# Layer 1's values two key blocks at a time beside layer 2, in a four-layer attention kernel

## The chip, the cores and the metric

The kernel runs on one core of a Trainium2 chip. Such a core has a matrix engine (TensorE, PE in the profile, with PEld for its loads of weights), a vector engine (VectorE, DVE), an engine for functions such as the exponential (ScalarE, ACT), a general one (GpSimd, POOL), and queues for transfers (SP issues nearly all of them here). Matrix products are written to a small memory of their own, PSUM; everything else is in SBUF. The metric is the time of one execution on the device in microseconds (us); the number given for a kernel is the median of several runs.

## The reference

The input x is four images of 64 x 64 pixels with 64 channels, all float32. Four layers follow one another, and each is an attention of every pixel over pixels of the same image, with a residual:

```python
# layer 0: q, k, v = x@Wq, x@Wk, x@Wv;  attn = softmax(q k^T, over keys)
out = einsum('bmn,bmc->bnc', attn, v);  x = gamma*out + x
# layer 1: theta = x@w_theta (8 columns); phi, g = maxpool2(x@w_phi), maxpool2(x@w_g)  (8 and 32 columns)
attn = softmax(einsum('bnd,bmd->bnm', theta, phi));  x = x + sigma*((attn g)@w_o + b_o)
# layer 2: group norm of 32 groups, q, k, v; softmax over keys; projection; + residual
# layer 3: group norm of 8 groups, q, k, v; softmax over keys; projection; + the normed input
```

Layers 0, 2 and 3 have 4096 queries and 4096 keys of 64 channels per image. Layer 1 pools its keys to 1024, and its queries and keys have only 8 channels, its values 32. Its four weights are first divided by an estimate of their largest singular value.

## The kernel before

All the work is written for one core, in an order fixed by hand (`tc.manual_schedule()`, L623): each engine carries out its instructions in the order in which the program issues them. The semaphores between engines follow from what reads and writes which tile.

Images lie channel by channel, two halves of 64 channels on the 128 partitions. Tiles come from pools (L625 to L627): `x` for what is as large as an image (8 KB a partition; the images themselves, q, k, v, layer 1's th, pg and its sums zacc1), `p` for exponentials (4 KB a partition), `ps_s` with two PSUM buffers of 128 x 1024 for scores and for everything else that is short-lived, and `ps_a` with four banks of 128 x 512 for accumulated outputs. A tile that is asked for when all buffers of its pool are taken waits for the last reader of one of them.

The large attentions (layers 0, 2 and 3) run one after another. Each is a loop of 64 steps, `step()` (L816). In layers 2 and 3 (`attention`, L1270) a step issues, in this order: two units of scores (`first`, matmuls at L1286 into both buffers of `ps_s`, each followed by an exponential on ACT, L1291, and a sum on DVE, L1297), and then the values' products of two units of an earlier step (`then`, L1321, into two `ps_a` banks).

The small work runs beside these loops as a generator that yields at named places (`background`, L782; `advance`, L806): MID lies between the two units of values, LATE in the middle of the second one, END after the step. At LATE the second unit of values is split by columns into two halves (`parts`, L846): the first half, then the background's piece, then the second half. When the second unit is a chunk's first or last key block, it isn't split, and the background's piece comes behind it.

Layer 1 is such a background. For images 1, 2 and 3 it runs beside layer 2 of the image before (L1777, L1783, L1789, with `bank=True`), and for image 0 beside layer 0 of image 1 (L1774, `bank=False`). Its loop (L1202 to L1217) goes over 16 units (two halves j of the queries, eight key blocks k each), in n = 0 to 16, one n at a LATE:

- `scores` (L1112) issues eight matmuls (L1120; the trace counts each float32 matmul twice, so 16) that fill both buffers of `ps_s`, and two exponentials on ACT (L1126) that empty them into two tiles of `p`. The array of TensorE is tiled 32 x 64 for them, as the keys have only 8 channels.
- `add` (L1139) multiplies the exponentials of one unit by its values, four matmuls (L1146, 8 in the trace) in a tiling of 128 x 32, into one `ps_a` bank that collects all eight key blocks of a half. After the eighth block ACT copies the bank.
- `accumulate` (L1133) sums the exponentials on DVE (L1135, x2 per unit); beside layer 2 it is put off to the end of the step (`later`).

In each n of 1 to 15, `scores` of unit n is followed by `add` of unit n - 1; n = 0 has only scores, and n = 16 only the last `add`. With `bank=False` the `add` comes at END instead, into a `ps_s` buffer.

Of the kernel before, what the change touches and what calls it, by code (L numbers as in the profile page):

```python
# [597 lines left out]
def fast_path(tc: tile.TileContext, a: dict, out: bass.AP, bad, read_flag):  # L598
# [10 lines left out]
    x = a["x"]  # L609
# [10 lines left out]
    MID, ALONE, LATE, END = range(4)  # L620
# [2 lines left out]
    ctx.enter_context(tc.manual_schedule())  # L623
    pool = lambda name, bufs, **kw: ctx.enter_context(tc.tile_pool(name=name, bufs=bufs, **kw))
    const, small = pool("const", 1), pool("small", 2)  # L625
    x_p, p_p, z_p, o_p = pool("x", 13), pool("p", 14), pool("z", 2), pool("o", 2)
    ps_s, ps_a = pool("ps_s", 2, space=PSUM), pool("ps_a", 4, space=PSUM)  # L627

    s_tile = lambda: ps_s.tile([P, 1024], FP, tag="s", name="s")
# [432 lines left out]
    def layer1(on, st, bank):  # L1062
# [49 lines left out]
        def scores(j, k):  # L1112

            ss = [s_tile() for e in range(2)]
            n, d = divmod(k, 2)
            for m in range(2):
                for e in range(2):
                    for i in range(2):
                        r = slice((2 * e + i) * 32, (2 * e + i) * 32 + D8)
                        nc.tensor.matmul(  # L1120
                            ss[e][half(m), chunk(i)], pgs[0 if e == d else 1][r, ds(n * P + m * C, C)],
                            th[r, chunk(i ^ j)], start=True, stop=True,
                        )
            ps[j, k] = pk = [p_tile() for e in range(2)]
            for e in range(2):
                nc.scalar.activation(pk[e], ss[e], AF.Exp)  # L1126
            if k == 0:
                return lambda: None
            if k == 1:
                zaccs[j] = x_tile("zacc1").rearrange("p (e f) -> p e f", e=2)  # L1130
            zs = [ps[j, 0][e] if k == 1 else zaccs[j][:, e, :] for e in range(2)]

            def accumulate():  # L1133
                for e in range(2):
                    nc.vector.tensor_tensor(zaccs[j][:, e, :], zs[e], pk[e], ALU.add)  # L1135

            return accumulate

        def add(j, k):  # L1139
            if k == (NK - 1 if bank else 0):  # L1140
                os[j] = o_tile("o1")
            if k == 0 and bank:
                accs[j] = acc_tile()
            acc = accs[j] if bank else s_tile()[:, 0:512]
            for q in range(4):
                nc.tensor.matmul(  # L1146
                    acc[quarter(q), :], g[:, k, :], ps[j, k][q // 2][:, chunk(q % 2)],
                    start=(k == 0 or not bank), stop=(k == NK - 1 or not bank),
                )
            if k > 0:  # L1150
                del ps[j, k]
            if k == 1:
                del ps[j, 0]
            if not bank and k > 0:
                nc.vector.tensor_tensor(os[j], os[j], acc, ALU.add)  # L1155
            elif not bank or k == NK - 1:
                nc.scalar.copy(os[j], acc)
# [44 lines left out]
        todo = [(j, k) for j in range(2) for k in range(NK)]  # L1202
        for n in range(len(todo) + 1):
            accumulate = None
            if n < len(todo):
                yield LATE
                accumulate = scores(*todo[n])
            if n:
                if not bank:
                    yield END  # L1210
                elif n == len(todo):
                    yield LATE
                add(*todo[n - 1])
            if accumulate and bank:
                later.append(accumulate)
            elif accumulate:
                accumulate()  # L1217
# [554 lines left out]
    layer0(s0)  # L1772
    drain()
    background(3.0, layer1("DVE", s0, False), before2("DVE", s0))  # L1774
    free = layer0(s1)
    drain()
    background(3.0, layer1("ACT", s1, True), before0("ACT", s2))  # L1777
    free = layer2(s0, free)
    drain()
    background(1.0, before2("DVE", s1), loads(s3))  # L1780
    free = layer0(s2)
    drain()
    background(3.0, layer1("ACT", s2, True), before0("ACT", s3))  # L1783
    free = layer2(s1, free)
    drain()
# [52 lines left out]
def conv_seq_kernel(tc: tile.TileContext, a: dict, out: bass.AP):  # L1838

    nc = tc.nc  # L1840
    with tc.tile_pool(name="flag", bufs=1) as flag:
        bad = flag.tile([1, 1], I32, name="bad")
        n_bad = fast_path(tc, a, out, bad, lambda: nc.values_load(
            bad[0:1, 0:1], min_val=0, max_val=128, skip_runtime_bounds_check_because="it is a count of 128 partitions"
        ))
        with tc.If(n_bad > 0):
            general_path(tc, a, out)
# [37 lines left out]
```

## Time and profile before

| | us |
|---|---|
| median of three runs (lowest, highest) | 2929.19 (2929.1, 2929.22) |
| the profiled execution, its own time | 2929.51 |
| its span, from the first to the last instruction | 2927.8 |
| PE busy | 2896.2 |
| DVE busy | 1869.1 |
| ACT busy | 1799.6 |
| stretches with layer 1 beside layer 2, near | 563 to 666, 1059 to 1161, 1555 to 1658 |
| PE, DVE, ACT busy in those three together (308 us) | 305.81, 253.09, 208.26 |
| a usual step there; a step of layer 2 without layer 1 | 5.64; 3.43 |

The profile is of one execution. Its page gives each engine's busy time, then the chain of waits that ended last (by engine and line), then groups of instructions. The timeline lists instructions in order of time, and those alike and overlapping are merged, with their number behind an x. In brackets stands how long an engine was idle before, and what ended that. PE's instructions overlap: the time that a group costs is read from its start to the start of the next group. The granted clock of TensorE is 0.999 throughout.

### The profile page before, as it was taken

The page shows a single profiled execution, that of the slowest core. Times are in us where ns is not written, and L with a number is a line of the kernel's source. Part 1 is how long each engine was busy: PE and PEld are TensorE (multiplying, and loading weights), DVE is VectorE, ACT ScalarE, POOL GpSimd, SP SyncE. Part 2 cuts the span into 40 slices and gives each one's busy share as a digit, 9 for nine tenths or more (in the row PEclk, how much of TensorE's full clock was granted, in tenths as well). Part 3 has the DMA queues.
Part 4 walks back from the last instruction along what each step waited for, and adds up shares of the span by engine and source line. Part 5 has one row for each costly group of instructions (what it writes and reads, how often), then busy time and mean ns, then how long its engine had stood idle before and what let it go on. Part 6 is the DMA issues. An engine that isn't in the chain of part 4 may idle for free.

```text
span 2927.8 us, 66456 instructions
## 1 busy us (share of the span) xinstructions
PE 2896.2 (99%) x29413; PEld 1135.3 (39%) x29413; DVE 1869.1 (64%) x2145; ACT 1799.6 (61%) x2481; POOL 33.7 (1%) x33
## 2 busy tenths in 40 slices
PE   9999999999999999999999999999999999999998
PEld 3333233333444433344443334444344444443333
DVE  2112752589831078973017998888888877878878
ACT  5666666665566766556766655555555655655554
POOL 0000000000000000000000000000000000000000
PEclk9999999999999999999999999999999999999999
DMA  2010000000002000000000000000000000000000
GB/s 38 1 30 5 1 1 16 5 5 5 19 5 30 1 5 5 11 17 16 1 1 5 5 9 20 19 5 9 5 19 7 21 5 7 6 20 5 8 5 9
DMA packets 76776, 30.11 MB, mean 10 GB/s; under 512 B 70464, under 2 KB 74560, under 8 KB 75072
## 3 DMA queue, kind: packets, MB, share of 16 engines
q1 hardware_dynamic: 74224, 25.37, 4.6%
q8 instruction: 232, 3.80, 0.5%
q10 hardware_dynamic: 2256, 0.41, 0.1%
q14 instruction: 64, 0.52, 0.1%
HBM read 4.79 MB, written 4.19 MB: 3 GB/s over the span
## 4 chain that ended last, share of the span: by engine, by line
PE 93%; DVE 4%; ACT 1%; issue 1%; DVEq 0%; ACTq 0%
PE acc L1321 28%; PE s L1286 28%; PE s L999 15%; PE acc L1028 15%; DVE zacc L1297 3%; PE s L1120 2%; PE acc L1146 2%; ACT p L1126 1%; PE s L1146 1%; PE s L912 0%; PE s L891 0%; PE s L1417 0%; PE s L1092 0%; PE s L1465 0%; PE s L1437 0%
## 5 line engine op out<-in xcount | busy, mean ns | idle before, releaser
L1291 ACT ACTIVATE p<-s 128x1024 f32<-128x1024 f32 x1024 | 994.4, 1022 | 693.6 <-PE s L1286 666.9
L1297 DVE TENSOR_TENSOR zacc<-zacc,p 128x1024 f32<-128x1024 f32 x960 | 1174.3, 1223 | 182.5 <-ACT p L1291 119.3
L1321 PE MATMUL acc<-p,v 64*64 64x512 f32 (+1 forms) x8576 | 1008.7, 572 | 0.0
L1009 ACT ACTIVATE p<-s 128x1024 f32<-128x1024 f32 x480 | 486.9, 1020 | 115.0 <-PE s L999 114.9
L1321 PEld LDWEIGHTS acc<-p,v 64*64 64x64 f32 x8576 | 349.2, 133 | 532.9 <-issue 532.9
L1028 PE MATMUL acc<-p,vs 64*64 64x512 f32 (+1 forms) x4224 | 502.0, 578 | 0.0
L1286 PE MATMUL s<-q,k 64*64 64x512 f32 x2048 | 492.1, 591 | 2.1 <-ACT p L1126 2.1
L1286 PE MATMUL s<-q,xT 64*64 64x512 f32 x2048 | 490.5, 590 | 0.0
L999 PE MATMUL s<-xT,q 64*64 64x512 f32 x2048 | 487.9, 592 | 2.5 <-DVE mean L1353 0.7
L999 PE MATMUL s<-xT,q_swapped 64*64 64x512 f32 x2048 | 488.1, 592 | 0.3 <-DVE o L1155 0.3
L1286 PE MATMUL s<-q,k_swapped 64*64 64x512 f32 x2048 | 481.2, 591 | 2.1 <-DVE xT L1471 2.1
L1286 PE MATMUL s<-q,h_swapped 64*64 64x512 f32 x2048 | 479.5, 590 | 0.5 <-DVE mean L1353 0.2
L1011 DVE TENSOR_REDUCE all_z<-z 128x1 f32<-128x4 f32 x128 | 20.1, 157 | 607.3 <-ACT p L1009 607.1
L1028 PEld LDWEIGHTS acc<-p,vs 64*64 64x64 f32 x4224 | 174.2, 133 | 264.7 <-issue 262.9
L1286 PEld LDWEIGHTS s<-q,h_swapped 64*64 64x64 f32 x2048 | 150.3, 133 | 135.6 <-issue 127.3
L1286 PEld LDWEIGHTS s<-q,k_swapped 64*64 64x64 f32 x2048 | 148.0, 133 | 140.7 <-issue 86.2
L1286 PEld LDWEIGHTS s<-q,xT 64*64 64x64 f32 x2048 | 150.7, 133 | 133.0 <-issue 127.1
L999 PEld LDWEIGHTS s<-xT,q_swapped 64*64 64x64 f32 x2048 | 146.9, 133 | 140.2 <-issue 111.2
L999 PEld LDWEIGHTS s<-xT,q 64*64 64x64 f32 x2048 | 144.7, 133 | 140.1 <-issue 108.9
L1286 PEld LDWEIGHTS s<-q,k 64*64 64x64 f32 x2048 | 148.6, 133 | 116.8 <-issue 98.2
L1017 ACT ACTIVATE vs<-v,all_r 128x64 f32<-128x64 f32 x256 | 89.0, 348 | 158.4 <-PE acc L1028 81.0
L1126 ACT ACTIVATE p<-s 128x1024 f32<-128x1024 f32 x128 | 124.1, 1021 | 82.8 <-PE s L1120 82.8
(215 smaller groups left out, 1322.7 us busy)
## 6 DMA issues: line engine op xcount, KB each, us to landing
k_swapped<-k SPq DMA_DIRECT2D x8, 512.0 KB, 6.3
residual<-turned SPq DMA_DIRECT2D x128, 32.0 KB, 1.8
h_swapped<-xT SPq DMA_DIRECT2D x8, 512.0 KB, 6.3
out_dram<-turned SPq DMA_DIRECT2D x60, 64.0 KB, 2.0
xin<-in_x_dram SPq DMA_DIRECT2D x12, 256.0 KB, 6.6
q_swapped<-q SPq DMA_DIRECT2D x6, 512.0 KB, 7.0
pg<-pg SPq DMA_DIRECT2D x8, 128.0 KB, 2.3
xin<-in_x_dram SPq DMA_DIRECT2D x12, 64.0 KB, 2.2
```

The costliest lines, as they stand in the source:

```text
L999: nc.tensor.matmul(s[half(e), chunk(i)], queries(m, i, e), k[half(i), chunk(c)], start=True, stop=True)
L1009: nc.scalar.activation(p, s, AF.Exp, accum_out=z)
L1011: nc.vector.tensor_reduce(zsum[:, m : m + 1], zs.pop(m), AX.X, ALU.add)
L1017: nc.scalar.activation(vs, v[:, m, :], AF.Copy, scale=rz[:, m : m + 1])
L1028: nc.tensor.matmul(acc[c][half(i), cols], scaled[t][half(e), :], ps[NC * m + c][half(e), chunk(i)][:, cols], start=(m == 0 and not second) ...
L1120: nc.tensor.matmul(ss[e][half(m), chunk(i)], pgs[0 if e == d else 1][r, ds(n * P + m * C, C)], th[r, chunk(i ^ j)], start=True, stop=True,)
L1126: nc.scalar.activation(pk[e], ss[e], AF.Exp)
L1146: nc.tensor.matmul(acc[quarter(q), :], g[:, k, :], ps[j, k][q // 2][:, chunk(q % 2)], start=(k == 0 or not bank), stop=(k == NK - 1 or not ...
L1286: nc.tensor.matmul(s[half(e), chunk(i)], k[(j + i) % 2][half(i), ds(j // 2 * P + e * C, C)], q[half(i), chunk(c)], start=True, stop=True,)
L1291: nc.scalar.activation(p, s, AF.Exp)
L1297: add = lambda: nc.vector.tensor_tensor(zaccs[c], p0, p, ALU.add)
L1321: nc.tensor.matmul(accs[c][e][half(i), cols], v[half(e), j, :], p[half(e), chunk(i)][:, cols], start=(j == 0), stop=(j == NB - 1),)
```

## The change

Where layer 1 runs beside layer 2, `add` is called for two units in succession at every even n (n = 2, 4, ..., 16, for units n - 2 and n - 1), behind the scores of that n, and not at all at odd n. The exponentials of an even unit are thus kept a step longer. The pool of exponentials has 16 buffers for 14, the pool of images 12 for 13 (the same space in all: 8 KB a partition less, 8 KB more). Layer 1 of image 0 (`bank=False`) is as before, except that the condition is written the other way round.

```diff
-    x_p, p_p, z_p, o_p = pool("x", 13), pool("p", 14), pool("z", 2), pool("o", 2)
+    x_p, p_p, z_p, o_p = pool("x", 12), pool("p", 16), pool("z", 2), pool("o", 2)
...
             if n < len(todo):
                 yield LATE
                 accumulate = scores(*todo[n])
-            if n:
-                if not bank:
-                    yield END
-                elif n == len(todo):
+            if n and not bank:
+                yield END
+                add(*todo[n - 1])
+            elif n and n % 2 == 0:
+
+                if n == len(todo):
                     yield LATE
-                add(*todo[n - 1])
+                for unit in todo[n - 2 : n]:
+                    add(*unit)
             if accumulate and bank:
                 later.append(accumulate)
             elif accumulate:
```

## Prediction

> **What bounds the kernel now.** I read the page first (busy shares, the chain of waits, the costliest groups), then the timeline of TensorE beside layer 2, then that of all engines there.
>
> ```profile
> span 2927.8 us, 66456 instructions
> PE 2896.2 (99%) x29413; PEld 1135.3 (39%) x29413; DVE 1869.1 (64%) x2145; ACT 1799.6 (61%) x2481; POOL 33.7 (1%) x33
> ...
> PE 93%; DVE 4%; ACT 1%; issue 1%; DVEq 0%; ACTq 0%
> ```
>
> The reader is to see that TensorE (PE) is busy for 99% and carries 93% of the chain: what an edit adds to PE, or leaves PE waiting for, is added to the time. So I ask of each step beside layer 2 how long it is on PE and why. The first timeline is PE alone, in the first two steps in which layer 1's loop runs beside layer 2 (columns: start, length, engine, line, operation; an entry's length includes the overlap with the next, so I go by differences of starts).
>
> ```profile
> 564.02 1.11 PE L1120 MATMUL s<-th,pg 8*64 8x512 f32 x16
> 565.07 0.66 PE L1321 MATMUL acc<-p,v 64*64 64x256 f32 x8
> 566.29 0.65 PE L1286 MATMUL s<-q,k 64*64 64x512 f32 x2 [0.56 <-ACT p L1126]
> ...
> 568.11 1.47 PE L1321 MATMUL acc<-p,v 64*64 64x512 f32 x16
> 569.51 1.11 PE L1120 MATMUL s<-th,pg 8*64 8x512 f32 x16
> 570.55 1.07 PE L1146 MATMUL acc<-p,pg 128*32 128x512 f32 x8
> 571.55 0.66 PE L1321 MATMUL acc<-p,v 64*64 64x256 f32 x8
> 572.03 0.60 PE L1286 MATMUL s<-q,k 64*64 64x512 f32 x2
> ...
> 573.75 1.47 PE L1321 MATMUL acc<-p,v 64*64 64x512 f32 x16
> 575.15 1.11 PE L1120 MATMUL s<-th,pg 8*64 8x512 f32 x16
> ```
>
> The step from 564.02 is the loop's n = 0: scores only, there is no earlier unit to add. The step from 569.51 is n = 1, the usual one: scores (L1120, 1.04), then one key block's values (L1146, 570.55 to 571.55, 1.00), the rest of layer 2's pass (L1321, 0.48), its next scores (L1286, 1.72), and 1.40 of pass: 5.64 us. The n = 0 step is without the 1.00 of L1146, and yet it lasts 569.51 - 564.02 = 5.49 us. Where the 1.00 went stands in brackets: PE waited for the exponentials (ACT p L1126). The same place with all engines:
>
> ```profile
> 565.21 1.94 ACT L1126 ACTIVATE p<-s 128x1024 f32<-128x1024 f32 x2 [1.26 <-PE s L1120]
> ...
> 567.20 0.14 PEld L1286 LDWEIGHTS s<-q,k_swapped 64*64 64x64 f32 x2 [0.71 <-ACT p L1126]
> ...
> 576.34 1.94 ACT L1126 ACTIVATE p<-s 128x1024 f32<-128x1024 f32 x2 [1.26 <-PE s L1120]
> ...
> 578.33 0.14 PEld L1286 LDWEIGHTS s<-q,k_swapped 64*64 64x64 f32 x2 [0.50 <-ACT p L1126]
> ```
>
> There are two score buffers (ps_s). Layer 1's scores fill both, and layer 2's next scores need them back from ACT, whose two exponentials take 1.94 us. The first comes back 1.22 us after the scores' end (565.07 to 566.29). In the usual step L1146 and the pass cover these 1.22 us (1.00 + 0.48 = 1.48); without L1146 only 0.48 covers them. A second place says the same: at n = 9 layer 2 has no half pass left to put there.
>
> ```profile
> 615.05 1.11 PE L1120 MATMUL s<-th,pg 8*64 8x512 f32 x16
> 616.09 1.06 PE L1146 MATMUL acc<-p,pg 128*32 128x512 f32 x8
> 617.32 0.65 PE L1286 MATMUL s<-q,k 64*64 64x512 f32 x2 [0.16 <-ACT p L1126]
> ...
> 619.14 1.47 PE L1321 MATMUL acc<-p,v 64*64 64x512 f32 x16
> ...
> 620.54 0.69 PE L1120 MATMUL s<-th,pg 8*64 8x512 f32 x8
> ```
>
> Here L1146 alone stands in the gap, and it is again 1.22 to 1.23 us (616.09 to 617.32): the wait is ACT's, whatever PE does meanwhile.
>
> **The change part by part.** Each of layers 1 of images 1, 2 and 3 runs n = 0 to 16 beside a layer 2. No multiplication is added or removed; each odd n loses its L1146 group, each even n from 2 to 16 gets a second one.
>
> *Odd n, 1 to 15.* The step takes the shape of n = 0: scores, half pass, wait for ACT. From the scores' end to the next full pass, n = 0 takes 1.22 + 1.82 = 3.04 (565.07 to 568.11) and n = 1 takes 1.00 + 0.48 + 1.72 = 3.20 (570.55 to 573.75). So the removed 1.00 us saves 0.16. I use the step lengths, 5.64 - 5.49 = 0.15. For seven of the eight odd n that is -1.05. At n = 9 L1146 lies wholly within the wait for ACT, and its removal saves nothing. Bounds: at most 1.00 saved each, if no wait came; at least 0.
>
> *Even n, 2 to 16.* Eight times one more L1146 group directly behind one of the same shape. Of the 1.00 of a group, two rounds of four parallel multiplications stream; a round is 1.72 / 4 = 0.43 by L1286 (sixteen multiplications, four at a time), so 0.86 streams and 0.14 is the change of the array's tiling (64*64, 8*64, 128*32). The second group has its predecessor's tiling and pays the 0.86. Bounds: 0.86, as PE streams no faster in any row here, and 1.00, the whole group. I take 0.86, since L1286 and L1321 in the rows above follow their own kind without a gap. Nothing hides it: in the usual step the next scores start 1.48 us after L1120's end, later than ACT's 1.22 asks, so PE is not waiting there and the addition goes straight into the step. 8 x 0.86 = +6.88.
>
> Sum for one layer 1: 6.88 - 1.05 = +5.83; for three, +17.5 us.
>
> [...]
>
> *The waits.* L1146 of an even n waits for exponentials one and two steps old; ACT ended those at least a step before, so no wait is added; layer 1's PSUM bank is taken at even n, a step later than now. Queued behind the longer L1146 on PE are the half pass and layer 2's scores; ACT and DVE get the latter 0.86 us later. ACT has 3.88 of work in a 5.64 step and DVE 4.82, so they catch up. In an odd step DVE has the same 4.82 in 5.49, which still fits. No DMA is issued, moved or passed on any queue by this edit.
>
> *16 exponential buffers for 14.* The earlier unit of a pair, two tiles, is held a step longer, which takes up the two new buffers beside layer 2; elsewhere they are spare. ACT waits for VectorE's sum (DVE zacc L1297), which holds such buffers, in 9 places, 12.4 us in all, all after 1990 us, when layer 1 is over. PE loses time at one of them, the 2.20 instead of 1.72 of L1286 at 2044.52: a gain of 0.5 at most, and 0 to that I take as -0.5. At the others PE's steps beside are 1.72, so nothing is to be had.
>
> *12 image buffers for 13.* Counting tiles from first to last use in the code's order, at most 12 are alive: the four images, q, k, k_swapped and v of layer 2 (8), th, pg and two zacc1 (12). So there is room, but none spare. The slot that the second zacc1 takes has been free since before its layer 1 began. I take 0. Bounds: 0, since one buffer fewer makes nothing earlier, and, at the three places that reach 12, each time the longest hole that PE shows after the start, 2.00 us (from 1743.96): +6.0.
>
> **Total.** The profiled execution took 2929.51 us (span 2927.8, 1.7 around it), 0.3 above the median 2929.19. +17.5 - 0.5 = +17.0; on the median 2946.2 us. About 0.2% (5.9 us) can be told from no change.
>
> **The rivals.**
>
> *The wait for ACT is covered after all (not slower).* The one mechanism: layer 2's scores don't wait in odd steps. An odd step then saves its whole 1.00, and a layer has 8 x (0.86 - 1.00) = -1.1, in all -3.4: 2925.8, no measurable change. It decides from the point where the 0.74 us of uncovered wait (1.22 - 0.48) shrinks under 0.14. For it: the odd step's ACT has its predecessor's exponentials done early. Against it: so it has at n = 0 (ACT was idle for 1.26 before), and all three layers show the wait there. 4%.
>
> *The second group is not streamed.* Each costs 1.00: 8 x 1.00 - 1.05 = 6.95 a layer, +20.9 - 0.5: 2949.6. For it: no row here has two L1146 groups in succession. Against it: eight weight loads of one group are done within 0.16 us, far ahead of the second round. 7%.
>
> *Image buffers run short.* The main case and up to 6.0 more: 2952.2. For it: 12 of 12 in use. Against it: the reused slots were last read long before. 5%.
>
> *Odd steps save more than n = 0 shows,* say half of the removed 1.00: 7 x -0.5 + 6.88 = 3.4 a layer, +10: 2939.3. Only n = 0 speaks for the size, and it has no VectorE sum beside it (DVE 2.60 us busy there against 4.82). 2%.
>
> **How the numbers follow.** The main case has 80%, 2943 to 2949: each of its terms 15% up or down. The range leaves out the first and the fourth rival and the worst of the third and takes in the second: 2942 to 2951. The four rivals have 18%; the last 2% are for a gain that no row suggests. Faster by over 0.2% needs 5.9 us, more than the first rival gives: those 2%. Within 0.2%: the first rival's 4%. Slower: 94%.
>
> **What would show it.** In the changed profile: L1146 in groups of 16 in every second step, lasting 1.86 to the next line; odd steps 5.49 with PE L1286 waiting for ACT p L1126, 21 more such waits near 0.56; even steps 6.50. A wait of PE or ACT for image tiles would show the third rival. I am wrong if odd steps fall to about 4.64, or if the time moves outside the stretches near 563 to 666, 1059 to 1161 and 1555 to 1658 us.

## The result

The changed kernel takes 2946.23 us (median of four runs, 2945.2 to 2947.37) against 2929.14 us before: a ratio of 1.0059, 95% interval 1.0046 to 1.0072. That is 17.1 us slower; 2946.2 was forecast. The profiled execution took 2946.95 us, its span 2945.1.

The page of the changed kernel: TensorE's work is the same 29413 instructions and its busy time nearly so (2896.2 before), in a longer span. The shares of the chain say little: PE has 95% here and had 93% before, but also 96% in the run e1 and 92% in e2 below, whose steps are those of before and of the changed kernel.

```profile
span 2945.1 us, 66460 instructions
...
PE 2899.0 (98%) x29413; PEld 1124.7 (38%) x29413; DVE 1868.8 (63%) x2145; ACT 1800.4 (61%) x2481; POOL 33.8 (1%) x33
...
PE 95%; ACT 2%; DVE 2%; issue 1%; DMA 0%; ACTq 0%; DVEq 0%
...
L1289 PE MATMUL s<-q,k 64*64 64x512 f32 x2048 | 494.8, 594 | 17.1 <-ACT p L1126 17.1
```

The last line is that of layer 2's scores (L1289 now, L1286 before; L1324 was L1321, L1120 and L1146 are as they were). Its last two columns are the idle time of PE just before it and what ended it: 17.1 us of waiting for layer 1's exponentials, where it was 2.1. The list of PE's waits has 27 of them, 6 before: 21 more, seven for each layer 1, and the one at n = 9 longer (1.15 us for 0.16). That the time grew by 17.1 us too is coincidence: the new waiting is 15.0 us, and PE's busy time rose as well, by 2.8 us.

The timeline of PE in a pair, n = 2 and n = 3 of the first layer 1 beside layer 2:

```profile
574.48 1.11 PE L1120 MATMUL s<-th,pg 8*64 8x512 f32 x16
575.53 1.92 PE L1146 MATMUL acc<-p,pg 128*32 128x512 f32 x16
577.38 0.66 PE L1324 MATMUL acc<-p,v 64*64 64x256 f32 x8
577.86 0.59 PE L1289 MATMUL s<-q,k 64*64 64x512 f32 x2
...
579.58 1.47 PE L1324 MATMUL acc<-p,v 64*64 64x512 f32 x16
580.98 1.11 PE L1120 MATMUL s<-th,pg 8*64 8x512 f32 x16
582.02 0.66 PE L1324 MATMUL acc<-p,v 64*64 64x256 f32 x8
583.24 0.65 PE L1289 MATMUL s<-q,k 64*64 64x512 f32 x2 [0.56 <-ACT p L1126]
...
585.07 1.47 PE L1324 MATMUL acc<-p,v 64*64 64x512 f32 x16
586.47 1.11 PE L1120 MATMUL s<-th,pg 8*64 8x512 f32 x16
```

The even step lasts 580.98 - 574.48 = 6.50 us, with 1.85 for two groups of values (575.53 to 577.38). The odd one lasts 586.47 - 580.98 = 5.49, with the wait in brackets: 1.22 from the end of layer 1's scores (582.02) to layer 2's next scores (583.24). A pair is 11.99, and two usual steps before were 11.28.

To see where the time came from, the starts of all 768 rounds of scores of the large attentions can be set against those of before; the difference rises in the three stretches beside layer 2 alone, but for single steps of 0.05 us. In this profile it rises by 7.27, 5.45 and 5.64 us there, and falls by 0.37 at one step near 2062 us (2044 before). Of the first, 1.64 us are a thing of their own, in the section on what was not expected; a later profile without it (label after_again) has 5.65, 5.42 and 5.67.

### The profile page after: what moved, and what is told of

Same layout as the page of the kernel before. It is cut to its first block, busy times and chain, and to the rows that moved or that the text cites. A ratio compares the mean times of both kernels' runs of the same rounds, so it can differ in the third digit from the quotient of the medians.

```text
span 2945.1 us, 66460 instructions
## 1 busy us (share of the span) xinstructions
PE 2899.0 (98%) x29413; PEld 1124.7 (38%) x29413; DVE 1868.8 (63%) x2145; ACT 1800.4 (61%) x2481; POOL 33.8 (1%) x33
## 4 chain that ended last, share of the span: by engine, by line
PE 95%; ACT 2%; DVE 2%; issue 1%; DMA 0%; ACTq 0%; DVEq 0%
PE s L1289 29%; PE acc L1324 29%; PE s L999 15%; PE acc L1028 15%; PE s L1120 2%; PE acc L1146 2%; ACT p L1126 2%; DVE zacc L1300 1%; PE s L1146 1%; PE s L912 0%; PE s L891 0%; PE s L1420 0%; ACT p L1294 0%; PE s L1192 0%; PE s L1092 0%
## 5 line engine op out<-in xcount | busy, mean ns | idle before, releaser
L1324 PE MATMUL acc<-p,v 64*64 64x512 f32 (+1 forms) x8576 | 1007.7, 572 | 0.0
L1324 PEld LDWEIGHTS acc<-p,v 64*64 64x64 f32 x8576 | 345.5, 133 | 537.0 <-issue 537.0
L1289 PE MATMUL s<-q,k 64*64 64x512 f32 x2048 | 494.8, 594 | 17.1 <-ACT p L1126 17.1
L1289 PE MATMUL s<-q,xT 64*64 64x512 f32 x2048 | 489.5, 589 | 0.0
L1289 PE MATMUL s<-q,k_swapped 64*64 64x512 f32 x2048 | 484.0, 594 | 2.1 <-DVE xT L1474 2.1
L1289 PE MATMUL s<-q,h_swapped 64*64 64x512 f32 x2048 | 479.3, 589 | 0.2 <-DVE v L1445 0.2
L1289 PEld LDWEIGHTS s<-q,h_swapped 64*64 64x64 f32 x2048 | 148.8, 133 | 136.7 <-issue 128.7
L1289 PEld LDWEIGHTS s<-q,xT 64*64 64x64 f32 x2048 | 149.0, 133 | 134.6 <-issue 128.3
L1289 PEld LDWEIGHTS s<-q,k_swapped 64*64 64x64 f32 x2048 | 144.6, 133 | 143.3 <-issue 98.6
L1289 PEld LDWEIGHTS s<-q,k 64*64 64x64 f32 x2048 | 145.1, 133 | 139.0 <-issue 97.8
```

What stands on the lines that cost most here:

```text
L1289: nc.tensor.matmul(s[half(e), chunk(i)], k[(j + i) % 2][half(i), ds(j // 2 * P + e * C, C)], q[half(i), chunk(c)], start=True, stop=True,)
L1324: nc.tensor.matmul(accs[c][e][half(i), cols], v[half(e), j, :], p[half(e), chunk(i)][:, cols], start=(j == 0), stop=(j == NB - 1),)
```

## The experiments

Two theories stood against each other. The one of the prediction: beside layer 2 a group of values is nearly free, as it stands in the time in which ACT empties the two score buffers; taken from an odd step it leaves a wait, put into an even step it costs itself. The rival: a group costs its own time on TensorE wherever it stands, and the loss is from elsewhere (the pools, a slow second group).

**The pools alone, and the pairs alone.** The first kernel is the one before with the pools of the change, the second the changed one with the pools before.

```diff
 # e1_pools_only, against before
-    x_p, p_p, z_p, o_p = pool("x", 13), pool("p", 14), pool("z", 2), pool("o", 2)
+    x_p, p_p, z_p, o_p = pool("x", 12), pool("p", 16), pool("z", 2), pool("o", 2)
 # e2_pairs_only, against the changed kernel
-    x_p, p_p, z_p, o_p = pool("x", 12), pool("p", 16), pool("z", 2), pool("o", 2)
+    x_p, p_p, z_p, o_p = pool("x", 13), pool("p", 14), pool("z", 2), pool("o", 2)
```

> The kernel before with only the pools changed (12 image buffers, 16 of exponentials); values one key block at a time as before. Theory (the loss is in the odd and even steps, the pools do nearly nothing): about 2928.8 us, the 0.4 us less from the one step near 2044 us in which ACT waits for a buffer of exponentials. Rival (12 image buffers are short, and part of the +17 us is theirs): over 2932 us, with PE or ACT waiting in the layers before 2 and 3.

> The changed kernel with the pools of before (13 and 14): the pairs alone. Theory: 0.4 us above the changed kernel's 2945.4 to 2947, as only the step near 2044 us comes back; even steps 6.50, odd steps 5.49. Rival (the pairs need the 16 buffers): ACT waits for buffers of exponentials beside layer 2 and the time is over 2950 us.

e1 measured 2928.4 us beside 2928.66 of before (ratio 0.9998, 0.9989 to 1.0007); e2 2947.37 (1.0062, 1.0046 to 1.0077). In the first, steps beside layer 2 are as before (5.64, two in each layer 5.67 or 5.68), and the difference to before moves by -0.35 at the step near 2044 us; in e2 the -0.37 of the changed kernel is missing, the pairs are 5.49 and 6.50, and the three stretches give 7.29, 5.43 and 5.66 us. ACT's timeline in e2 still has the wait for a buffer that 16 buffers take away:

```profile
2060.21 1.95 ACT L1294 ACTIVATE p<-s 128x1024 f32<-128x1024 f32 x2 [1.43 <-PE s L1289]
2063.81 1.02 ACT L1294 ACTIVATE p<-s 128x1024 f32<-128x1024 f32 x1 [1.66 <-DVE zacc L1300]
2065.13 1.02 ACT L1294 ACTIVATE p<-s 128x1024 f32<-128x1024 f32 x1 [0.30 <-DVE zacc L1300]
```

and in e1 it is gone:

```profile
2041.74 1.94 ACT L1291 ACTIVATE p<-s 128x1024 f32<-128x1024 f32 x2 [1.50 <-PE s L1286]
2045.23 2.06 ACT L1291 ACTIVATE p<-s 128x1024 f32<-128x1024 f32 x2 [1.55 <-PE s L1286]
```

So the pools are worth 0.4 us of gain, 12 image buffers cost nothing, and the pairs do without 16 buffers beside layer 2. All of the loss is the pairs'.

**A group added at each odd n.** The group is one of the same kind and size; its product is counted twice in the output.

```diff
 # e3_odd_filled, against the changed kernel
-            if k == 0 and bank:
+            if k == 0 and bank and j not in accs:
                 accs[j] = acc_tile()
...
-                    start=(k == 0 or not bank), stop=(k == NK - 1 or not bank),
+                    start=not bank, stop=(k == NK - 1 or not bank),
...
+        def again(j, k):
+            if j not in accs:
+                accs[j] = acc_tile()
+            for q in range(4):
+                nc.tensor.matmul(
+                    accs[j][quarter(q), :], g[:, k, :], ps[j, k][q // 2][:, chunk(q % 2)],
+                    start=(k == 0), stop=False,
+                )
...
                 for unit in todo[n - 2 : n]:
                     add(*unit)
+            elif n:
+                again(*todo[n - 1])
```

> The changed kernel with an extra group of values at each odd n: the earlier unit of the pair is multiplied there too, so that it is counted twice in the output; 24 groups of work more for TensorE. Theory (odd steps are set by ACT giving back the two score buffers, and a group there is covered): odd steps go from 5.49 to 5.64 only, n = 9 stays at 5.49, so 21 x 0.15 = 3.2 us more, about 2948.6 us. Rival (each group costs its own time wherever it stands): 24 x 0.86 to 24 x 1.00, 2966 to 2970 us.

Measured 2948.12 us (1.0066, 1.005 to 1.0081), and by the starts 6.65, 6.42 and 6.65 us for the three layers: 1.0 more than in after_again's profile for eight more groups. PE's timeline of n = 1 and 2:

```profile
568.44 1.11 PE L1120 MATMUL s<-th,pg 8*64 8x512 f32 x16
569.48 1.07 PE L1206 MATMUL acc<-p,pg 128*32 128x512 f32 x8
570.48 0.66 PE L1335 MATMUL acc<-p,v 64*64 64x256 f32 x8
...
574.08 1.11 PE L1120 MATMUL s<-th,pg 8*64 8x512 f32 x16
575.12 1.92 PE L1146 MATMUL acc<-p,pg 128*32 128x512 f32 x16
```

The extra group (L1206) takes its 1.00 (569.48 to 570.48), and the step is 5.64 instead of 5.49: 24 groups, each of 1.00 us, cost 3 us. The rival's 2966 to 2970 is out.

**A group left out at each odd n.** The same from the other side: every second key block's values are missing.

```diff
 # e4_odd_left_out, against before
-            if k == 0 and bank:
+            if k == 1 and bank:
                 accs[j] = acc_tile()
...
-                    start=(k == 0 or not bank), stop=(k == NK - 1 or not bank),
+                    start=(k == 1 or not bank), stop=(k == NK - 1 or not bank),
...
-                add(*todo[n - 1])
+                if bank and n % 2:
+                    if todo[n - 1][1]:
+                        del ps[todo[n - 1]]
+                else:
+                    add(*todo[n - 1])
```

> The kernel before without the group of values at odd n, even n as before: every second key block's values are left out of layer 1 beside layer 2, so 24 groups of work less. Theory: odd steps 5.49 for 5.64, n = 9 unchanged, 21 x 0.15 = 3.2 us less, about 2926.0 us. Rival (a group costs its own time): 24 x 1.00 = 24 us less, about 2905 us.

Measured 2926.23 us beside 2928.66 (0.9992, 0.9982 to 1.0001). Whole runs of this kernel are 4.6 us apart, and the profiled one, of 2924.0 us, is 1.78 us ahead of before after ten steps (the start, in the last section; the other runs have no trace), so the stretches say more: 1.03, 1.27 and 1.04 us less by the starts, 7 x 0.15 = 1.05 expected. (The 1.27 holds 0.22 of a single odd step of before at 1137 us.) 24 groups less on the busiest engine are worth 3 us.

```profile
578.50 1.11 PE L1120 MATMUL s<-th,pg 8*64 8x512 f32 x16
579.54 0.66 PE L1325 MATMUL acc<-p,v 64*64 64x256 f32 x8
580.76 0.65 PE L1290 MATMUL s<-q,k 64*64 64x512 f32 x2 [0.56 <-ACT p L1126]
...
583.99 1.11 PE L1120 MATMUL s<-th,pg 8*64 8x512 f32 x16
585.03 1.07 PE L1146 MATMUL acc<-p,pg 128*32 128x512 f32 x8
586.03 0.66 PE L1325 MATMUL acc<-p,v 64*64 64x256 f32 x8
```

**The cause itself made shorter.** So far the wait follows from what PE does. Here PE's work stays and ACT's is cut.

```diff
 # e6_half_exponentials, against the changed kernel
-                nc.scalar.activation(pk[e], ss[e], AF.Exp)
+                if bank and k % 2:
+                    nc.scalar.activation(pk[e][:, 0:512], ss[e][:, 0:512], AF.Exp)
+                    nc.gpsimd.memset(pk[e][:, 512:1024], 0.0)
+                else:
+                    nc.scalar.activation(pk[e], ss[e], AF.Exp)
```

> The changed kernel in which ACT takes the exponentials of the odd units of layer 1 beside layer 2 for half of the columns only, and GpSimd writes zeros into the other half: half of these exponentials are left out. TensorE's work is the same. Theory (ACT giving back the score buffers sets the odd steps): ACT's two instructions shorten from 1.02 to about 0.59 us each (that of the 512 columns of L1330), the first buffer comes back after 0.79 instead of 1.22 us and the second no longer late, so odd steps fall from 5.49 to about 4.95, 24 x 0.54 = 13 us less, about 2932.5 us (2930 to 2935). Rival (something on TensorE holds the odd steps): unchanged, 2945 to 2947 us.

Measured 2933.9 us (1.0015, 1.0006 to 1.0024) beside 2945.77 for the changed kernel on the same chip. All engines at n = 1:

```profile
567.03 1.11 PE L1120 MATMUL s<-th,pg 8*64 8x512 f32 x16
...
568.08 0.66 PE L1328 MATMUL acc<-p,v 64*64 64x256 f32 x8
568.22 1.08 ACT L1127 ACTIVATE p<-s 128x512 f32<-128x512 f32 x2 [1.31 <-PE s L1120]
...
568.87 0.65 PE L1293 MATMUL s<-q,k 64*64 64x512 f32 x2
...
570.64 1.47 PE L1328 MATMUL acc<-p,v 64*64 64x512 f32 x16
...
572.04 0.23 PEld L1120 LDWEIGHTS s<-th,pg 8*64 8x64 f32 x16 [0.38 <-ACT p L1298]
```

ACT's two take 1.08 us, the first buffer is back 0.79 us after the scores (568.08 to 568.87), as worked out from the 0.59 of another line, and the step lasts 5.01 (572.04 - 567.03). That is 0.48 less here and 0.46 to 0.49 in the others, a little under the 0.54 expected, since layer 2's scores still take 1.77 (568.87 to 570.64) and not 1.72. By the starts the three stretches are 1.91, 1.66 and 1.88, together 11.3 us less than in after_again's profile, where 13 were expected. With the same work on TensorE the odd step follows ACT: the cause is shown.

**Unit 8 kept at n = 9.**

```diff
 # e5_n9_kept, against the changed kernel
+            elif n == 9:
+                add(*todo[8])
             elif n and n % 2 == 0:
...
-                for unit in todo[n - 2 : n]:
+                for unit in todo[n - 2 + (n == 10) : n]:
```

> The changed kernel, but at n = 9 unit 8 is added there, as before the change, and n = 10 adds unit 9 alone. In the profile of the changed kernel PE stands idle for 1.15 us at n = 9, and after one of the three such places the granted clock was 0.5 for 3.4 us. Theory (that idle time brings the clock down): n = 9 keeps 5.49 us, n = 10 loses 0.86, so 2.6 us less, about 2942.8 us, no stretch of half clock beside layer 2, and runs within 0.5 us of each other. Rival (the clock falls for another reason, the half-microsecond waits of all odd steps for one): runs still 1.5 us and more apart.

> The changed kernel again, beside the two others on the same chip. Theory: 2945.2 us in runs without a stretch of half clock and 1.7 us more for each such stretch, so a spread over 1 us. Rival (the spread was of that chip or hour): all runs within 0.5 us.

e5 measured 2943.59 us (2941.9 to 2943.76; ratio 1.0049, 1.0035 to 1.0062), the changed kernel again 2945.77 (2945.1 to 2947.52; 1.0059, 1.0045 to 1.0073). Of the step lengths the expectation held for n = 9, which is 5.49 with the group as without it; n = 10 fell by 0.61 only (10.05 to 9.44) and not by 0.86, for the reason given below under even n. The spread tells nothing: e5's runs are 1.9 us apart and not within 0.5, but on this chip those of before are 1.6 apart too. The profile of e5 has no fall of the clock beside layer 2, that of after_again has none either; so this run left the matter of the clock open, and the next one was made for it.

**The hole of n = 9 at every odd n.**

```diff
 # e7_more_holes, against the changed kernel
             if n < len(todo):
-                yield LATE
+                if bank and n % 2:
+                    yield MID
+                    yield END
+                else:
+                    yield LATE
                 accumulate = scores(*todo[n])
```

> The changed kernel with the scores of each odd n put behind the whole pass instead of into its middle, as it is at n = 9: nothing covers ACT's return of the score buffers, so PE stands idle for 1.15 us in each of the 24 odd steps instead of in 3, and the odd steps last about 5.49 + 0.43 = 5.92 us. Without any fall of the clock: 2945.4 + 21 x 0.43 = 2954.4 us. Theory (a hole of 1.15 us brings the clock to a half for 3.4 us where it meets the right moment, as it did at 2 of the 12 holes of this size that the profiles show at n = 9 so far): some 1 to 8 stretches of granted clock 0.5 in the profile, each 1.65 us, so 2956 to 2968 us. Rival (the falls have nothing to do with these holes): none or one such stretch, 2953 to 2956 us.

Measured 2978.1 us (1.0171, 1.0154 to 1.0188), above either range. A pair lasts 12.41 us where the clock doesn't fall, 0.42 more than 11.99, as expected; but the profile has 14 stretches of granted clock 0.5 beside layer 2, not 1 to 8. With them the sum is right: 2945.4 + 21 x 0.42 + 14 x 1.65 = 2977.3, the profiled run took 2977.53. The columns of the windows are: from and to, length, busy time of PE, PEld, DVE, ACT and POOL, granted clock, DMA.

```profile
568.00:571.41 3.41, 2.26 (x30) 0.44 (x24) 1.81 (x2) 1.67 (x3) 0.00 (x0) 1.00 0.00 0
571.41:574.82 3.41, 3.41 (x20) 1.00 (x16) 0.96 (x1) 1.85 (x3) 0.00 (x0) 0.50 0.01 2
...
581.65:585.06 3.41, 2.31 (x28) 0.39 (x20) 2.27 (x2) 1.73 (x3) 0.00 (x0) 1.00 0.02 5
585.06:588.47 3.41, 3.35 (x40) 1.16 (x48) 1.14 (x1) 2.90 (x4) 0.00 (x0) 1.00 0.00 0
```

The first hole (from 569.91, 1.15 us) is followed by half clock, the second (from 583.97) isn't. All falls of the clock lie whole multiples of 3.4133 us apart (those at 571.41 and 598.72 us of this profile eight of them, 27.31 us). Counted from the points of that grid, the 14 holes that start 1.05 to 2.19 us behind such a point are all followed by half clock from the next point on, and of the ten others (0.86, or 2.23 and later) none. The twelve holes at n = 9 in the profiles of after, after_again, e2 and e4 split in the same way: the two that start 1.59 and 1.85 us behind a point are followed by half clock, the ten others (0.17 to 0.93, or 2.81 and later) aren't. Layer 1's scores start 1.11 us ahead of each hole, and a hole is 1.15 to 1.21 us long. So, to within 0.1 us, half clock followed in these profiles where the scores and the hole lay in one interval of the grid together, and didn't where a point of the grid cut through either: 36 of 36 holes. The rival, no connection, is out.

**Pairs beside layer 0.** Image 0's layer 1 has no PSUM bank: its group takes a score buffer, and waits for ACT itself (0.56 us before the group at 302.40 us of before). There pairs have no cover to lose.

```diff
 # e8_pairs_layer0, against before
-    x_p, p_p, z_p, o_p = pool("x", 13), pool("p", 14), pool("z", 2), pool("o", 2)
+    x_p, p_p, z_p, o_p = pool("x", 12), pool("p", 16), pool("z", 2), pool("o", 2)
...
+        def pair(j, k):
+            acc = s_tile()[:, 0:512]
+            for kk in (k - 1, k):
+                for q in range(4):
+                    nc.tensor.matmul(
+                        acc[quarter(q), :], g[:, kk, :], ps[j, kk][q // 2][:, chunk(q % 2)],
+                        start=(kk == k - 1), stop=(kk == k),
+                    )
+                del ps[j, kk]
+            if k == 1:
+                os[j] = o_tile("o1")
+                nc.scalar.copy(os[j], acc)
+            else:
+                nc.vector.tensor_tensor(os[j], os[j], acc, ALU.add)
...
-            if n:
-                if not bank:
-                    yield END
-                elif n == len(todo):
+            if n and not bank:
+                if n % 2 == 0:
+                    yield END
+                    pair(*todo[n - 1])
+            elif n:
+                if n == len(todo):
                     yield LATE
                 add(*todo[n - 1])
```

> The kernel before with pools of 12 and 16, and pairs where layer 1 runs beside layer 0 (image 0) instead: there a group of values has no PSUM bank of its own, takes a score buffer and waits for ACT itself (0.56 us idle on PE before each of 16 groups at 296 to 385 us), so that it covers nothing. Two units are summed in one score buffer at every even n. Theory: odd steps fall from 6.45 to about 5.49 us and even ones rise by 0.86 to 7.31, a pair 12.80 for 12.90: 8 x 0.1 = 0.8 us less, with the 0.4 us of the pools 1.2 us less than before, about 2928.0 us against 2929.2, and never slower. Rival (pairs lose here as well, as beside layer 2): 0.70 us a pair more, 2934 us.

Measured 2927.61 us beside 2928.92 (0.9996, 0.9987 to 1.0005): in the direction expected, and not to be told from no change by the times. The starts tell it: -1.08 us over that stretch, 0.70 of it in the first seven pairs and the rest at the loop's end.

```profile
299.51 1.11 PE L1120 MATMUL s<-th,pg 8*64 8x512 f32 x16
300.56 0.66 PE L1028 MATMUL acc<-p,vs 64*64 64x256 f32 x8
301.78 0.65 PE L999 MATMUL s<-xT,q 64*64 64x512 f32 x2 [0.56 <-ACT p L1126]
...
305.00 1.11 PE L1120 MATMUL s<-th,pg 8*64 8x512 f32 x16
306.05 0.66 PE L1028 MATMUL acc<-p,vs 64*64 64x256 f32 x8
307.27 1.92 PE L1163 MATMUL s<-p,pg 128*32 128x512 f32 x16 [0.56 <-ACT p L1126]
```

The wait of 0.56 stands in both kinds of step, and only the second group costs less: the two take 1.85 us (307.27 to 309.12), where one of before takes 1.00 (302.40 to 303.40), and a pair of steps lasts 12.80 for 12.90 us. Of all kernels with the reference's work this is the lowest, but nothing here beats the kernel before measurably.

## Why the prediction was right

*What bounds the kernel.* Right: the whole loss lies in the stretches named, on PE, and the new waits are the 21 named.

*Odd n.* The 0.15 us read from n = 0 held: 5.49 at n = 1, 3, 7 and 15, 5.50 at n = 5, 5.54 at n = 11; n = 13, which lasts longer, saved 0.13 (9.55 to 9.42); n = 9 saved nothing. That this is ACT's return of the two buffers, and not an accident of the first step, e3, e4 and e6 show each in another way.

*Even n.* Two groups in succession take 1.85, so the second costs 0.85 to 0.86, and the rival of 1.00 falls; that the 0.14 it lacks is the change of tiling stays the author's estimate. One of the eight was mis-sized: n = 10 rose by 0.61 and not 0.86. Before, layer 2's scores of the next step took 1.96 there and not 1.72, as the loads of their weights waited for a buffer that DVE's reduction of sums (L1245) held (0.90 us idle before the load at 627.67, and 0.9 in the other two layers):

```profile
626.62 0.60 PE L1286 MATMUL s<-q,k 64*64 64x512 f32 x2
...
628.58 0.61 PE L1321 MATMUL acc<-p,v 64*64 64x512 f32 x4
```

Behind the longer step they take 1.72 (631.43 to 633.15 in the changed profile): that wait is gone. The prediction had no such term, some 0.25 for each layer.

*A layer 1.* 5.83 was predicted; measured 5.65, 5.42 and 5.67. The 5.42 has the 0.22 that before lost at 1137 us.

*The pools.* -0.5 for exponentials was -0.37, at the step named. 0 for images was 0. The rival of short image buffers falls with e1. Its bound was too wide: the 2.00 us from 1743.96 run from one start to the next, and PE was idle for 1.41 of them.

*The sum.* Three layers gave 16.7 and not 17.5, the pools -0.4 and not -0.5. That makes about 2945.5 us. The median agrees with the forecast to the tenth all the same, but the profiled run lost another 1.64 us to the clock at n = 9, of which the prediction said nothing, and the profiles differ by up to 2.4 us at their start: that agreement is chance within 1 us, the 17 us are not. (The sums of the first and the fourth rival, 2925.8 and 2939.3, leave out the -0.5 of the pools.)

*The first rival* (the wait is covered) fell: its condition was that the 0.74 us of uncovered wait shrink under 0.14; it stayed at 0.74.

## What to carry to other kernels

Work on the busiest engine may still be free where it stands in a wait for buffers: with two score buffers and ACT's 1.94 us for them, no step with layer 1's scores was shorter than 5.49 us until e6 cut ACT's part, and with the group of values it is 5.64. So before work is gathered to save changes of tiling (here a group took 1.00 us behind another tiling and 0.85 behind its own), look in the trace for a step that already lacks it, here n = 0, and read what takes its place. Two steps made unequal cost the wait of the one and the work of the other (a pair 11.99 us here, 11.28 before).

## What was not expected of the hardware

*Half clock after a hole of 1.15 us.* At n = 9 the changed kernel has no half pass of layer 2 to set behind the scores, so PE stands idle for 1.15 us. PE's timeline and two windows of the changed kernel there:

```profile
617.37 1.11 PE L1120 MATMUL s<-th,pg 8*64 8x512 f32 x16
...
619.63 0.75 PE L1289 MATMUL s<-q,k 64*64 64x512 f32 x2 [1.15 <-ACT p L1126]
...
620.17 1.07 PE L1289 MATMUL s<-q,k 64*64 64x512 f32 x2
...
624.50 1.11 PE L1120 MATMUL s<-th,pg 8*64 8x512 f32 x16
```

```profile
616.60:620.05 3.45, 2.30 (x28) 0.44 (x24) 0.61 (x1) 1.76 (x3) 0.00 (x0) 1.00 0.00 0
620.05:623.47 3.42, 3.42 (x20) 1.00 (x16) 2.46 (x3) 2.34 (x4) 0.00 (x0) 0.50 0.00 0
```

The step takes 7.13 instead of 5.49: a round of four multiplications 0.86 instead of 0.43 us from 620.05 to 623.47, 1.64 us lost. The same is in the profile of e2 at this n, and not in after_again's nor at the other two n = 9 of either; e7 shows on which places in a grid of 3.4133 us it depends. Idle time alone doesn't decide: the holes at 1121.64 and 1623.17 us of the changed kernel's profile last 1.15 us as well, and the clock behind them is 1.00. PE's busy share doesn't either: in after_again's profile the hole at n = 9 lies within one interval of the grid, with PE busy for 2.26 of its 3.41 us, as in e7's interval from 568.00 that half clock followed, and the clock stayed full:

```profile
618.52:621.93 3.41, 2.26 (x28) 0.72 (x24) 0.72 (x2) 3.16 (x4) 0.00 (x0) 1.00 0.00 0
```

There a point of the grid (618.52) cuts through the scores ahead of the hole (617.58 to 618.69). Why the place of the scores matters no run shows.

*The start.* The clock of 0.999 given for the kernel before is the mean of the execution: its profile grants the full clock from 14.5 to 2922.7 us, the profile of e4 from 4.9 us on, the others from times between. After ten steps e4 is 1.78 us and e6 (full clock from 5.0) 2.37 us ahead of before; the other kernels, with 11.6 to 14.4 us, are 0.93 to 0.08 ahead, in the order of these times, so the lead goes with the clock. A difference of 1 us between whole runs of such kernels says little, and the comparison of starts stretch by stretch says much.
